# The first batch of a decoder layer with its projections in another order

## The chip, the cores and the metric

The kernel runs on one core of one Trainium2 chip. Its time is the device time of one execution in microseconds (us). Three timed runs of the kernel before gave 1556.1, 1555.15 and 1556.22; the median is 1556.1. One further execution was profiled: it took 1556.36, and the profile's span is 1554.6.

A core has five engines that run beside each other, each through its own list of instructions in order: TensorE (PE, matrix products; its weight loads are listed as PEld), VectorE (DVE), ScalarE (ACT), GpSimd (POOL) and SyncE (SP, which here issues most DMAs). Results of PE go to PSUM, and DVE or ACT carry them to SBUF.

## What is computed

A pre-norm decoder layer over `x` of 8 batches, 256 tokens, 1024 features: self-attention, cross-attention and a feed-forward network, each added to its input. The change touches only the self-attention of the first batch. Its weights are taken by their signs, and each output row is scaled by the mean absolute weight:

```python
def bitnet_linear(x, weight, scale_param):
    s = jnp.maximum(jnp.mean(jnp.abs(weight), axis=1), 1e-08)
    binary_w = jnp.sign(weight / s[:, None])
    y = jnp.einsum('bsi,oi->bso', x, binary_w)
    y = y * (s * scale_param)[None, None, :]
    return jnp.nan_to_num(y, nan=0.0, posinf=1000000.0, neginf=-1000000.0)

q = bitnet_linear(hidden_states, q_weight, q_scale)   # 32 heads of 32
k = bitnet_linear(hidden_states, k_weight, k_scale)   # 8 heads of 32, each used four times
v = bitnet_linear(hidden_states, v_weight, v_scale)
scores = jnp.einsum('bhqd,bhkd->bhqk', q, k) / np.sqrt(HEAD_DIM)
attn = jax.nn.softmax(scores, axis=-1)
out = jnp.einsum('bhqk,bhkd->bhqd', attn, v)
return bitnet_linear(out, o_weight, o_scale)
x = x + attention(layernorm(x))
```

## The kernel before

**Weight blocks.** The four weight matrices come in 20 blocks of 128 output rows by 1024 (512 KB): two of k, two of v, eight of q, eight of o. The list `blocks` (L243 to L262) gives their order, and "block 5" or "weight 5" means the sixth of that list. Before: k0, k1, q0, q1, v0, v1, q2 to q7, o0 to o7. Each block needs

- a load by SP (`weight_load`, L273): one DMA for k and v, four for q, eight for o. Eight buffers hold blocks (`room`); `after` says which later block takes the buffer of an earlier one, and `weight_next` issues that load after the earlier block's sum;
- a turn (`weight_turn`, L303): eight 128x128 transposes on PE into two PSUM banks, and two passes of ACT that write the signs;
- a sum (`weight_sum`, L292): a DVE reduction over 1024 columns with a small operation behind it, and three small operations on POOL that put the row's scale factor into a column of `scol`.

**Scale tables.** The outputs of q and k are scaled row by row from `scol` by ACT. Those of v and o need the factors along the free dimension: `scale_part` (L318) lets POOL multiply the identity by each column (`dg`, in its `ahead`), lets PE multiply ones by these (`ps_d`, L332) and lets DVE copy the result to `v_sc` or `o_sc` (L333).

**Projections.** A chunk is 128 outputs for 256 tokens: 16 matrix products over `xh` and `xl`, the upper and lower part of the normalised, transposed input. `first_chunk` (L414) makes a single chunk with its clean-up on DVE alone: five operations, six for k. `proj_T` (L386) makes two chunks as two parts; with the second, ACT scales both out of the PSUM bank into `y` (L406), and `nan_to_num` (L345) cleans up on DVE (two operations) and POOL (`tmp` L350, an addition L351), with a predicated copy on DVE (L355) that is not issued at once: `settle` (L172), called at each part, issues it two parts later. Three PSUM banks in rotation (`bank`, L107) serve turns, projections, tables and transposes; a bank is free again when its last reader is done.

**Steps.** A batch has eight steps, one for four heads. `step` (L676) issues the scores (PE, 16 products into four banks), the row maxima `nm` (DVE, L686), four times four transposes of the step before's probabilities with ACT's copies (`turned`, L518), and then the parts which `self_plan` (L1134) gives to this step; among them, by a budget in us that each part carries, come ACT's eight exponentials (L705). When the first four are issued, `over_sums(0)` is called, and after all eight `over_sums(1)`: a DVE reciprocal each, and then two heads divided by their sums. The table `BY` (L1112) says by whom: "D" is DVE, "P" is POOL. For the first batch it is DDDD, PPPD, PPPD, PPPP, PPPD, PPPD, DDDD, PPPD. A step ends with the product of the transposed probabilities of the step before with v (`po`, L581), which the step after it carries to `oh` and `ol`. Parts that have something to prepare (`ahead`) prepare it when the part in front of them is run, or at the start of the step if they are among its first two or are marked `soon`.

**The first batch** also holds the turning of the weights. Before the first step (from L1249): the loads of x and of eight blocks, the layernorm's statistics, turn 0, the layernorm (transposes L1268, casts L1270, subtractions L1273), turn 1, the sums 0 and 1, then k0, turn and sum 2, k1, turn and sum 3, q0, q1, and the load of the second batch's x. `self_plan` for batch 0 then gives the steps v, q2 to q7, the other turns, the tables, the second batch's layernorm (`ln_parts`, four parts, each with `xn` on DVE as its `ahead`, four transposes on PE, a cast on ACT and a subtraction `xl` on DVE) and the second batch's k, v and q0 to q3. The second batch's moments are prepared in pieces on DVE (`idle`, L125; run by a credit of time).

All five engines are under a hand-written order: each carries out its instructions as the program issues them.

Of the kernel before, what the change touches and what calls it, by code (L numbers as in the profile page):

```python
# [35 lines left out]
def decoder_layer(  # L36
# [24 lines left out]
    nc = tc.nc  # L61
# [3 lines left out]
    EC = E // P  # L65
# [170 lines left out]
    ps = bank([P, 20], "ps_p")  # L236
# [8 lines left out]
    def block(put, t, col, w, q=False, o=False):  # L245
        a = State()
        a.put, a.t, a.col, a.rows, a.q, a.o = put, t, col, w, q, o
        blocks.append(a)

    def columns(dst, t):  # L250
        return lambda e0: dst[:, e0 : e0 + 4, t * P : (t + 1) * P]

    for t in range(2):
        block(columns(kT_w, t), t, 8 + t, kw)
    for c in range(2):
        block(columns(qT_w[c], 0), c, c, qw, q=True)
    for t in range(2):
        block(columns(vT_w, t), t, 10 + t, vw)
    for c in range(2, EC):
        block(columns(qT_w[c], 0), c, c, qw, q=True)  # L260
    for t in range(EC):
        block(columns(oT_w, t), t, 12 + t, ow, o=True)  # L262

# [39 lines left out]
    def weight_turn(i):  # L303

        a = blocks[i]
        for h in range(2):
            nc.scalar.activation(
                a.put(4 * h), four_T(a.w[:, h * 512 : (h + 1) * 512], "ps_w"), AF.Sign
            )

    def weight_next(i):

        weight_turn(i)
        weight_sum(i)
        for k in after.get(i, []):
            weight_load(k)

    def scale_part(col0, n, dst, soon=False):  # L318

        box = {}  # L320

        def ahead():
            box["dg"] = wk_.tile([P, n, P], F32, tag="xn", name="dg", bufs=2)
            for k in range(n):
                nc.gpsimd.tensor_scalar_mul(
                    box["dg"][:, k, :], ident, scol[:, col0 + k : col0 + k + 1]
                )

        def main():
            ps = bank([P, n, P], "ps_d")  # L330
            for k in range(n):
                nc.tensor.matmul(ps[:, k, :], ones, box["dg"][:, k, :], start=True, stop=True)  # L332
            nc.vector.tensor_copy(dst, ps.rearrange("p k c -> p (k c)"))  # L333

        return Part(0.3 * n, main, ahead, soon)

    def weight(i):
        return Part(1.1, lambda: weight_next(i))
# [795 lines left out]
    def self_plan(b):  # L1134
        st = sts[b]
        if b == 0:
            nxt = sts[1]
            v0 = v_parts(st)
            ln, k, v = ln_parts(nxt, 1), k_parts(nxt), v_parts(nxt)
            return [  # L1140
                [weight(4), weight(5), v0[0], weight(6), weight(7)]
                + [scale_part(10, 2, v_sc), v0[1]],
                mixed(q_parts(st, 2) + q_parts(st, 4), [weight(8), weight(9), weight(10)]),
                [weight(11)] + q_parts(st, 6) + [weight(12)],
                [weight(13)] + ln[:2] + [weight(14)] + ln[2:],
                k[:1] + [weight(15)] + k[1:],
                mixed(v, [weight(16), weight(17)]),
                mixed(q_parts(nxt, 0), [weight(18), scale_part(12, 4, o_sc[:, 0:512], True)])
                + [weight(19)],
                mixed(q_parts(nxt, 2), [scale_part(16, 4, o_sc[:, 512:1024])]),  # L1150
            ]
        o = o_all(sts[b - 1])
        if b + 1 < B:
            nxt = sts[b + 1]
            ln = ln_parts(nxt, b + 1)
            return [
                q_parts(st, 4) + q_parts(st, 6),
                mixed(o[0], ln[:2]),
                mixed(o[1], ln[2:]),
                k_parts(nxt),  # L1160
                o[2] + v_parts(nxt),
                o[3],
                q_parts(nxt, 0),
                q_parts(nxt, 2),
            ]
        x0 = xts[0]
        ln = lnx_parts(x0)
        return [
            q_parts(st, 4) + q_parts(st, 6),
            o[0],  # L1170
            o[1],
            mixed(o[2], ln[:2]),
            mixed(o[3], ln[2:]),
            ctx_parts(x0, (act, dve)) + ckv_part(x0),
            cq_part(x0) + ckvT_part(x0),
            cqk_parts(x0, (dve, act)),
        ]
# [62 lines left out]
    with tc.manual_schedule(  # L1240
        engines={
            mybir.EngineType.PE,
            mybir.EngineType.DVE,
            mybir.EngineType.Activation,
            mybir.EngineType.Pool,
            mybir.EngineType.SP,
        }
    ):
        st = sts[0]  # L1249
        xb[0] = load_x(0)  # L1250
        for i in range(len(room)):
            weight_load(i)
        ln_moments(st, 0)
        need(st)
        weight_turn(0)
        st.xh = wk_.tile([P, EC, S], F32R, tag="xh", name="xh")
        st.xl = wk_.tile([P, EC, S], F32R, tag="xl", name="xl")
        lo = []
        for q in range(2 * TB):
            t, h = q // 2, q % 2  # L1260
            xn = wk_.tile([P, 512], F32, tag="p", name="xn0", bufs=4)
            nc.vector.tensor_scalar(
                xn, xb[0][t][:, h * 512 : (h + 1) * 512],
                st.mv[:, t, 0:1], st.rs[:, t : t + 1], ALU.subtract, ALU.mult,
            )
            ps = pss.tile([P, 4, P], F32, tag="pss", name="ps_t")
            for k in range(4):
                nc.tensor.transpose(ps[:, k, :], xn[:, k * P : (k + 1) * P], ident)  # L1268
            e4, t4 = slice(h * 4, (h + 1) * 4), slice(t * P, (t + 1) * P)
            nc.scalar.copy(st.xh[:, e4, t4], ps)  # L1270
            lo.append((st.xl[:, e4, t4], ps, st.xh[:, e4, t4]))
        for a in lo:
            nc.vector.tensor_sub(*a)  # L1273
        weight_turn(1)
        for i in range(2):
            weight_sum(i)
        for i in range(2):
            for k in after.get(i, []):
                weight_load(k)
        st.kT = wk_.tile([P, 2, S], F32, tag="kT", name="kT", bufs=2)  # L1280
        st.qT = wk_.tile([P, EC, S], F32, tag="qT", name="qT", bufs=2)
        for i in range(2):
            first_chunk(
                st, lambda e: kT_w[:, e, i * P : (i + 1) * P], 8 + i, st.kT[:, i, :], K_SCALE
            )
            weight_next(2 + i)
        for i in range(2):
            first_chunk(st, lambda e: qT_w[i][:, e, :], i, st.qT[:, i, :])
        xb[1] = load_x(1)

        prev = None
        for kind, sts_, plan, loads, extra, n in (
            (Self, sts, self_plan, self_loads, self_extra, EC),
            (Cross, xts, cross_plan, cross_loads, cross_extra, XH // 4),
        ):
            for b in range(B):
                ps_ = plan(b)
                for p in ps_:
                    queue.extend(p)
                for c in range(n):  # L1300
                    loads(b, c)
                    prev = step(kind(sts_[b], c), prev, len(ps_[c]), extra(b, c))


        pairs = [(fb, f) for fb in fbs for f in range(NF)]
        acs = {}

        def hidden_next(n):
            acs[n] = hidden(*pairs[n])

        prev.prev.early()
        pTs = [turned(p) for p in prev.p]
        prev.prev.late()
        fw.late = None
        hidden_next(0)
        prev.weighted(pTs)
        hidden_next(1)
        prev.early()
        prev.late()
        ffn_load_end()  # L1320
        fw.late = wt.tile([P, 2 * RC, W], F32, tag="vw", name="late")
        settle()
        settle()
        lag = 2
        for n in range(2, len(pairs) + lag):
            fb, f = pairs[n] if n < len(pairs) else (None, n)
            if fb is not None:
                hidden_next(n)
                if fb.i == 0 and f == 3:
                    x_leave(xts[B - 1])  # L1330
                elif idle:
                    idle.pop(0)()
                if fb.i + 1 < NB:
                    if f == 6:
                        ffn_x(fbs[fb.i + 1])
                    if f == 8:
                        hp = head_parts(fbs[fb.i + 1])
                        queue.extend(hp)
                        queue[0].ahead()
                    if 9 <= f < 9 + len(hp):  # L1340
                        run_part()
            m = n - lag
            down(*pairs[m], *acs.pop(m))
            if fb is not None and fb.i and 2 <= f < 2 + BT:
                tail(fbs[fb.i - 1], f - 2)
        for j in range(BT):
            tail(fbs[NB - 1], j)
# [34 lines left out]
```

## Time and profile before

| | value |
|---|---|
| median of three runs | 1556.1 us |
| the profiled execution | 1556.36 us |
| its span | 1554.6 us |
| PE busy in the span | 1510.9 us (97%) |
| DVE busy | 964.1 us (62%) |
| ACT busy | 799.8 us (51%) |
| POOL busy | 404.7 us (26%) |
| HBM read and written | 65.44 MB and 25.17 MB |

Steps of the first batch in that execution, by the start of their scores on PE and of their maxima on DVE (timeline):

| step | scores | maxima |
|---|---|---|
| 0 | 26.41 | 27.87 |
| 1 | 42.22 | 44.21 |
| 2 | 58.15 | 59.43 |
| 3 | 67.96 | 71.22 |
| 4 | 83.82 | 85.93 |
| 5 | 93.67 | 96.19 |
| 6 | 104.55 | 107.11 |
| 7 | 115.88 | 120.40 |
| second batch, 0 | 127.08 | 128.25 |

The page cuts the span into 40 slices of 38.9 us and gives each engine's busy share in tenths; the first batch lies in the first three and a bit. The first table's shares are means over the whole kernel, of which the first batch is a twelfth.

### The profile page before, as it was taken

What the parts mean: (1) busy time and instruction counts of PE and PEld (TensorE: products, weight loads), DVE (VectorE), ACT (ScalarE), POOL (GpSimd) and SP (SyncE); (2) the same over time, 40 slices, a digit from 0 to 9 for tenths busy, and PEclk for the clock granted to TensorE, in tenths of its full rate; (3) what the DMA queues carried; (4) which work ended last, traced back from release to release, by engine and by line L of the source; (5) the groups of instructions that cost most, each with busy time, mean ns of one, the idle gap of its engine ahead of it and who ended that gap; (6) DMA issues with size and microseconds to landing.
All of it is one profiled execution on the core that took longest, in us unless ns stands there. A gap on an engine that the chain in (4) does not pass through costs nothing.

```text
span 1554.6 us, 25703 instructions
## 1 busy us (share of the span) xinstructions
PE 1510.9 (97%) x9494; PEld 1014.8 (65%) x9494; DVE 964.1 (62%) x1880; ACT 799.8 (51%) x2448; POOL 404.7 (26%) x491
## 2 busy tenths in 40 slices
PE   6899999999999999999999999999999999999998
PEld 5777888788878786777778776544444444444443
DVE  7878999999989898766676665343233233423322
ACT  4677898989888888755565666311101111111110
POOL 2555443445354534022221111100020002001102
PEclk9989999999999999999999999999999999999999
DMA  8430020101020141211453311110001002000001
GB/s 233 67 82 26 18 69 28 55 29 67 17 69 29 60 150 44 86 42 61 154 187 132 113 61 77 48 54 0 0 41 68 1 0 108 0 1 27 28 0 54
DMA packets 65612, 92.78 MB, mean 60 GB/s; under 512 B 40218, under 2 KB 46160, under 8 KB 65360
## 3 DMA queue, kind: packets, MB, share of 16 engines
q1 hardware_dynamic: 60880, 74.37, 15.2%
q0 software_dynamic: 4608, 16.78, 2.7%
q8 instruction: 75, 1.23, 0.3%
q14 instruction: 49, 0.40, 0.1%
HBM read 65.44 MB, written 25.17 MB: 58 GB/s over the span
## 4 chain that ended last, share of the span: by engine, by line
PE 78%; DVE 10%; ACT 6%; DMA 2%; issue 1%; POOL 1%; SPq 1%; POOLq 0%; DVEq 0%; ACTq 0%
PE ps_h L1034 19%; PE ps_z L1078 9%; PE ps_pt L522 9%; PE ps_q L397 6%; PE ps_o L490 5%; ACT p L705 4%; PE s L619 4%; PE ps_p L1008 4%; PE po L642 4%; PE ps_o L1097 3%; PE s L543 3%; PE po L581 3%; DVE nm L686 2%; PE ps_o L659 2%; PE ps_q L848 2%; PE ps_qk L863 2%
## 5 line engine op out<-in xcount | busy, mean ns | idle before, releaser
L705 ACT ACTIVATE p<-s,nm 128x256 f32<-128x256 f32 x768 | 357.9, 517 | 0.4 <-DVE nm L686 0.4
L526 ACT COPY pT<-ps_pt 128x512 f32<-128x512 f32 x384 | 198.6, 598 | 178.1 <-PE ps_pt L522 177.3
L1046 ACT ACTIVATE sg<-ps_h,b_col 128x512 f32<-128x512 f32 (+1 forms) x88 | 59.7, 678 | 413.5 <-PE ps_h L1034 413.5
L686 DVE TENSOR_REDUCE nm<-s 128x2 f32<-128x512 f32 x384 | 237.3, 677 | 9.9 <-PE s L619 6.8
L1047 DVE SCALAR_TENSOR_TENSOR sg<-ps_h,b_col,sg 128x512 f32<-128x512 f32 (+1 forms) x88 | 64.9, 738 | 272.2 <-ACT sg L1046 272.2
L522 PE MATMUL ps_pt<-ident,p 128*128 128x128 f32 x1536 | 195.7, 278 | 4.8 <-DVE xl L343 3.2
L522 PEld LDWEIGHTS ps_pt<-ident,p 128*128 128x128 f32 x1536 | 164.4, 141 | 45.6 <-issue 25.5
L705 ACT ACTIVATION_READ_ACCUMULATOR p<-s,nm 128x1 f32 x768 | 190.9, 249 | 0.0
L1107 POOL TENSOR_TENSOR x2t<-x2t,y 128x512 f32<-128x512 f32 x32 | 40.6, 1267 | 480.3 <-DVE y L1105 480.3
L1078 PE MATMUL ps_z<-ac,u_sb 128*128 128x512 f32 x336 | 157.7, 593 | 0.0
L397 PE MATMUL ps_q<-xh,qT_w 128*128 128x256 f32 x496 | 121.8, 287 | 0.0
L397 PE MATMUL ps_q<-xl,qT_w 128*128 128x256 f32 x496 | 118.9, 281 | 0.0
L674 POOL TENSOR_TENSOR x1t<-x1t,y 128x256 f32<-128x256 f32 x64 | 47.5, 764 | 234.6 <-DVE y L667 234.6
L1078 PEld LDWEIGHTS ps_z<-ac,u_sb 128*128 128x128 f32 x336 | 61.9, 190 | 68.8 <-issue 68.8
L490 PE MATMUL ps_o<-oT_w,oh 128*128 128x512 f32 x256 | 105.9, 414 | 0.0
L350 POOL TENSOR_SCALAR tmp<-y 128x512 f32<-128x512 f32 x78 | 57.2, 733 | 183.7 <-DVE y L499 106.4
L490 PE MATMUL ps_o<-oT_w,ol 128*128 128x512 f32 x256 | 101.0, 395 | 0.0
L566 DVE TENSOR_SCALAR p<-p,sm 128x256 f32<-128x256 f32 x252 | 90.1, 414 | 8.0
L397 PEld LDWEIGHTS ps_q<-xh,qT_w 128*128 128x128 f32 x496 | 93.3, 188 | 1.6
L397 PEld LDWEIGHTS ps_q<-xl,qT_w 128*128 128x128 f32 x496 | 93.4, 188 | 0.0
L1034 PE MATMUL ps_h<-pT,w_ffn 128*128 128x512 f32 (+1 forms) x184 | 88.7, 577 | 0.0
L1034 PE MATMUL ps_h<-late,w_ffn 128*128 128x512 f32 (+1 forms) x184 | 88.7, 577 | 0.0
(159 smaller groups left out, 2737.0 us busy)
## 6 DMA issues: line engine op xcount, KB each, us to landing
xs<-in_x_dram SPq DMA_DIRECT2D x32, 512.0 KB, 4.1
x<-xs POOLq DMA_DIRECT2D x16, 512.0 KB, 3.0
x1t<-x SPq DMA_DIRECT2D x16, 512.0 KB, 5.2
c<-in_ctx_dram SPq DMA_DIRECT2D x16, 512.0 KB, 3.8
x<-x1t POOLq DMA_DIRECT2D x16, 512.0 KB, 3.8
x2t<-x SPq DMA_DIRECT2D x16, 512.0 KB, 5.8
out_dram<-x2t SPq DMA_DIRECT2D x16, 512.0 KB, 2.6
w<-in_L_attn_q_weight_dram SPq DMA_DIRECT2D x32, 128.0 KB, 5.9
```

Of the source, the lines that this page charges most:

```text
L397: nc.tensor.matmul(ps[:, i, :], w(i, e), x_[:, e, :], start=(e == 0 and x_ is st.xh), stop=(e == EC - 1 and x_ is st.xl),)
L490: nc.tensor.matmul(ps, o_[c // 4][:, c % 4, t * P : (t + 1) * P], oT_w[:, c, h * 512 : (h + 1) * 512], start=(c == 0 and o_ is st.oh), sto ...
L522: nc.tensor.transpose(ps[:, k, t * P : (t + 1) * P], p[:, t, k * P : (k + 1) * P], ident)
L526: nc.scalar.copy(pT, ps)
L566: nc.vector.tensor_scalar_mul(p, p, self.sm[:, t, j : j + 1])
L619: nc.tensor.matmul(s[2 * i + j][:, t, :], st.cqk[p0 : p0 + XD, 2 * c + i, t * P : (t + 1) * P], st.ckv[p0 : p0 + XD, :], start=True, stop= ...
L642: nc.tensor.matmul(self.po[XD * j : XD * (j + 1), i, :], self.st.ckvT[:, k, :], pTs[2 * i + j][:, k, :], start=(k == 0), stop=(k == TB - 1),)
L686: nc.vector.tensor_reduce(nm[:, j, :], s[j], AX.X, ALU.max, negate=True)
L705: nc.scalar.activation(cur.p[j][:, t, :], s[j][:, t, :], AF.Exp, bias=nm[:, j, t : t + 1], accum_out=cur.sm[:, t, j : j + 1],)
L1034: nc.tensor.matmul(ps[h * n : h * n + n], v1_of(r, i, f, n), fb.pT[:, r, h * w_ : (h + 1) * w_], start=(r == 0), stop=(r == RC - 1),)
L1047: nc.vector.scalar_tensor_tensor(sg[:m], hs[0][:m], bg, sg[:m], ALU.add, ALU.mult)
L1078: nc.tensor.matmul(fb.zs[r], fw.u2[f // 4][:n, f % 4, r * P : (r + 1) * P], ac[:n], start=(k == 0), stop=(k == NF - 1 and COPIES < 2),)
```

## The change

It has five parts.

1. The list of blocks is put in another order: k0, q0, q1, v0, v1, q2, q3, k1, q4 to q7, o0 to o7. Loads follow this order.
2. Before the first step only k0 and q0 are projected. The sum of block 0 (k0) moves ahead of the layernorm. Blocks 2 and 3 (q1, v0) are turned there, and block 2 is summed. The load that takes block 2's buffer is issued in step 0.
3. `weight_next` is split, so that sums and loads can be issued apart from turns (`weight_free`). In step 0, `turn_4` turns block 4, sums 3 and 4 and issues the loads behind them; blocks 5 and 6 are turned there, and their sums are issued at the end of the step (`sums`).
4. The parts are dealt out to the steps anew: q1 to step 0, the second k chunk to step 1, q4 and q5 to step 2, q6 and q7 to step 3 with the second batch's layernorm; the o blocks are turned a step later in part, and the second half of the o table is the last part of step 7.
5. The scale tables are copied from PSUM by ACT in place of DVE.

```diff
-    for t in range(2):
-        block(columns(kT_w, t), t, 8 + t, kw)
-    for c in range(2):
-        block(columns(qT_w[c], 0), c, c, qw, q=True)
+    def q_blocks(*chunks):
+        for c in chunks:
+            block(columns(qT_w[c], 0), c, c, qw, q=True)
+
+    K, V, Q = [0, 7], [3, 4], [1, 2, 5, 6, 8, 9, 10, 11]
+    block(columns(kT_w, 0), 0, 8, kw)
+    q_blocks(0, 1)
     for t in range(2):
         block(columns(vT_w, t), t, 10 + t, vw)
-    for c in range(2, EC):
-        block(columns(qT_w[c], 0), c, c, qw, q=True)
+    q_blocks(2, 3)
+    block(columns(kT_w, 1), 1, 9, kw)
+    q_blocks(4, 5, 6, 7)
...
+    def weight_free(i):
+        for k in after.get(i, []):
+            weight_load(k)
+
     def weight_next(i):
-
         weight_turn(i)
         weight_sum(i)
-        for k in after.get(i, []):
-            weight_load(k)
+        weight_free(i)
...
-            nc.vector.tensor_copy(dst, ps.rearrange("p k c -> p (k c)"))
+            nc.scalar.copy(dst, ps.rearrange("p k c -> p (k c)"))
...
+            def turn_4():
+                weight_turn(4)
+                weight_free(2)
+                for i in V:
+                    weight_sum(i)
+                    weight_free(i)
+
+            def sums():
+                for i in Q[2:4]:
+                    weight_sum(i)
+                    weight_free(i)
+
             return [
-                [weight(4), weight(5), v0[0], weight(6), weight(7)]
-                + [scale_part(10, 2, v_sc), v0[1]],
-                mixed(q_parts(st, 2) + q_parts(st, 4), [weight(8), weight(9), weight(10)]),
-                [weight(11)] + q_parts(st, 6) + [weight(12)],
-                [weight(13)] + ln[:2] + [weight(14)] + ln[2:],
-                k[:1] + [weight(15)] + k[1:],
-                mixed(v, [weight(16), weight(17)]),
-                mixed(q_parts(nxt, 0), [weight(18), scale_part(12, 4, o_sc[:, 0:512], True)])
-                + [weight(19)],
-                mixed(q_parts(nxt, 2), [scale_part(16, 4, o_sc[:, 512:1024])]),
+                [Part(2.0, lambda: q_chunk(1)), Part(0.9, turn_4), v0[0]]
+                + [Part(0.9, lambda i=i: weight_turn(i)) for i in Q[2:4]]
+                + [scale_part(10, 2, v_sc), v0[1], Part(0.0, sums)],
+                mixed(q_parts(st, 2), [weight(8), weight(7)])
+                + [Part(2.0, lambda: k_chunk(1)), weight(9)],
+                [weight(10)] + mixed(q_parts(st, 4), [weight(11)]),
+                q_parts(st, 6) + ln[:2] + [weight(12)] + ln[2:],
+                mixed(k, [weight(13), weight(14)]),
+                mixed(v, [weight(15), weight(16)]),
+                mixed(q_parts(nxt, 0), [weight(17), scale_part(12, 4, o_sc[:, 0:512], True)])
+                + [weight(18)],
+                mixed(q_parts(nxt, 2), [weight(19)]) + [scale_part(16, 4, o_sc[:, 512:1024])],
             ]
...
         weight_turn(0)
+        weight_sum(0)
+        weight_free(0)
...
         weight_turn(1)
-        for i in range(2):
-            weight_sum(i)
-        for i in range(2):
-            for k in after.get(i, []):
-                weight_load(k)
+        weight_sum(1)
+        weight_free(1)
...
-        for i in range(2):
+        def k_chunk(i):
             first_chunk(
                 st, lambda e: kT_w[:, e, i * P : (i + 1) * P], 8 + i, st.kT[:, i, :], K_SCALE
             )
-            weight_next(2 + i)
-        for i in range(2):
+        def q_chunk(i):
             first_chunk(st, lambda e: qT_w[i][:, e, :], i, st.qT[:, i, :])
+        k_chunk(0)
+        q_chunk(0)
+        for i in (2, 3):
+            weight_turn(i)
+        weight_sum(2)
         xb[1] = load_x(1)
```

## The prediction

> **What bounds the kernel now.** I read the page's slices first, then the busy time by stretch, then what TensorE (PE) waited for up to 160 us, then the timelines of DVE, ACT and POOL over the first batch. "Step c" is head group c of the first batch; "block" is a slice of weights in the plan's order.
>
> ```profile
> PE   6899999999999999999999999999999999999998
> DVE  7878999999989898766676665343233233423322
> ...
> 160.00:180.00 20.00, 20.00 (x180) 16.79 (x179) 17.42 (x38) 15.81 (x53) 9.57 (x9) 1.00 0.07 29
> ```
>
> After 160 us PE is full, and the diff touches nothing there. What counts is the first batch. Its steps' scores start (timeline of PE) at 26.41, 42.22, 58.15, 67.96, 83.82, 93.67, 104.55 and 115.88, the second batch's first at 127.08; a shift of that last one is the change in time.
>
> ```profile
> 30.00:40.00 10.00, 5.98 (x41) 5.32 (x41) 8.60 (x20) 5.87 (x21) 3.79 (x14) 0.91 0.79 178
> ...
> 70.00:80.00 10.00, 5.89 (x38) 4.32 (x35) 9.93 (x17) 8.28 (x24) 4.51 (x9) 0.79 0.08 12
> ...
> 34.70:38.20 3.50, 0.48 (x2) 0.30 (x2) 3.17 (x8) 1.17 (x4) 1.73 (x5) 1.00 0.64 99
> 38.20:41.60 3.40, 3.16 (x15) 3.15 (x15) 1.28 (x5) 0.00 (x0) 0.80 (x4) 0.51 0.73 114
> ```
>
> Columns: length, then busy PE, weight load, DVE, ACT, POOL, then PE's granted clock. In 70 to 80 DVE is full and PE is not: there the bound is DVE. After PE's idle stretch at 34.7 the clock is 0.51.
>
> ```profile
> PE ps_d L332 <- POOL dg L325: 3.3, 2, 3.0
> PE ps_t L163 <- DVE xn L155: 2.9, 3, 2.2
> PE ps_w L163 <- ACT y L406: 1.9, 2, 1.4
> ...
> 24.75 0.15 DVE L298 TENSOR_SCALAR s<-total 128x1 f32<-128x1 f32 x1
> 24.82 0.28 DVE L428 TENSOR_SCALAR qT<-y 128x256 f32<-128x256 f32 x1
> ...
> 27.87 2.48 DVE L686 TENSOR_REDUCE nm<-s 128x2 f32<-128x512 f32 x4
> ...
> 121.33 2.38 POOL L325 TENSOR_SCALAR dg<-ident,scol 128x128 f32<-128x128 f32 x4
> 123.66 3.10 POOL L559 TENSOR_TENSOR p<-p,sm 128x512 f32<-128x512 f32 x3
> ```
>
> The longest waits: 3.0 us for v's scale table, 2.2 for the layernorm, 1.4 for a PSUM bank held by y. q0's clean-up (24.82) stands behind a weight sum, so the first maxima come at 27.87. In step 7 the second o-table's dg (121.33) stands ahead of POOL's multiplications.
>
> **Prices** (spacings in the timelines). PE: chunk 2.0 (45.11 to 47.12), turn 0.8, scores 1.1, four transposes of p 1.9, po 1.0. DVE: sum 1.3 (15.78 to 17.09), clean-up of one chunk 1.65 (24.82 to 26.46), of K 1.8, maxima 2.4. ACT: exp 0.45, casts of a turn 1.0. POOL: p 1.02, dg 0.6, a block's scol 0.8. A DVE pair of p takes 1.9 beside POOL (50.99).
>
> **Prologue.** Block 0's sum falls into DVE's wait for rs (idle 1.15 before 10.25): 9.1 to 10.4, so xn starts 0.2 later; nothing else. q0 replaces k1 in the DMA queue: its last piece lands at 13.2 today (chain), earlier by k1's half megabyte then, and its turn is at 14.3. k0 on PE 15.3 to 17.3, q0 to 19.3; its scale factor is there by 18.3, so y at 19.75, clean-up after k0's 19.8 to 21.35. Scores 21.4: 5.0 earlier, but two chunks (4.0 of PE) are still owed.
>
> **Step 0.** Sum of block 2, then maxima 22.75 to 25.15; q1's clean-up to 26.75, v's sums to 29.5, p of pair 0 to 30.8, pair 1 to 32.1. POOL's dg is ready at 31.75 instead of 38.4, since only v's two sums stand ahead. PE loses some 1.4 and 0.8 to the banks of turns 5 and 6; table 32.3. No row shows ACT copying 128x256 from PSUM to a table: the cast of oh (0.37) and the copy of 128x512 (0.60) bound it, I take 0.4, off DVE's 0.42. v's second half ends at 34.25; DVE has v's part to 36.2, the two sums put off to 38.9. Scores of step 1 at 34.25 (8.0 earlier), maxima only at 38.9 (5.3 earlier).
>
> **Step 1.** The maxima, not PE, set the pace: exps 39.6 to 44.15, with turn 8's casts between, then y of q2, q3. Block 7's turn needs the bank that this y holds (the 1.4 us wait above, same rotation of banks): q's second chunk ends at 41.95, y at 45.0, so the wait grows to 3.05. Then k1 must follow its own turn at once: casts to 46.45, chunk to 48; its y waits on ACT for scol till 50.0. DVE: 2.4 maxima, 0.7 of v, three sums 4.0, pair 1.9, q 0.8, q's predicated copy 0.7, moments 2.1, K 1.8, waits 1: step 2's maxima at 54.4 (5.0 earlier; scores 50).
>
> **Step 2.** Two sums, a pair, one q: maxima of step 3 at 64.0, 7.2 earlier, with a sum and q6, q7's pass (2.8 of DVE) still owed.
>
> **Step 3** holds q6, q7 and the layernorm. Its p are "PPPP": POOL gets four multiplications (4.1) at the reciprocal, 68.5, then q's tmp 0.65 and add 1.3: 74.55. q's predicated copy is issued on DVE two parts after q, that is behind the first xl and ahead of the second xl, third xn, block 12's sum and fourth xn. DVE reaches it at 71.0 and stands 3.5 us; today no q ends in this step. All that is queued on DVE waits, and PE for it: idle 71.5 to 76.45, last transposes at 79. Maxima of step 4: 82.9, only 3.0 earlier, with two sums (2.6) owed.
>
> **SP's queue.** q6 and q7 now go behind the second batch's x and behind the sums of blocks 2 and 3 (22.7, 28.1); they are turned from 53 on. The load of block 13 waits for a sum put off, 37.6, and is turned in step 4; that of block 19 for block 15's sum, 99.7: eight DMAs (4.46 at 92.25) and 2.4 to land, 107, turned at 117. None is on the path, which costs nothing as long as these 10 us and more last.
>
> **The clock** goes down in both. The row: 2.23 us of idle ended at 74.29, and 74.30 to 82.00 ran at 0.60, the po after it took 1.86 for 1.0. The Trainium skill (TensorE: Matmul & The Clock Gate, Part 1: The HAM clock gate) speaks of half rate after at least one idle window of about 3.4 us. By its rule neither that stop nor the one before 37.72 would cost anything unless a whole window were idle, and step 7's term below would be 0 or 1.7; the trace shows a drop after 2.2 us, so it decides, and the term stays.
>
> **Steps 4 to 6.** Step 4 has a sum and turn more than today (10.3 to 11.5 of DVE): maxima of step 5 at 94.4, of step 6 at 104.5 (today 107.11). Step 6 keeps DVE busy for 13.29 today; without the o-table's copy (0.64, spacing 0.56) 12.7: maxima of step 7 at 117.2, 3.2 earlier, with one sum owed. ACT copies the table in 0.60 (row of pT) where it has room.
>
> **Step 7** now ends with the second o-table, and its dg is made ahead only when q's second half starts. From the maxima N: first four exps N+2.5, reciprocal N+2.95, POOL two p to N+5.0, block 19's scol to 5.8, third p (needs all exps, casts of turn 19 between them) to 6.85, dg to 9.25, PE's table N+9.5, po, scores N+10.5. Today it is 127.08 - 120.40 = N+6.7: 3.8 lost. PE itself is through its chunks at 120.0, so it stands some 4 us.
>
> **Sum.** 117.2 + 10.5 = 127.7 against 127.08: +0.6. PE's stop of 4 us brings a stretch at half clock; the row (po 1.86 for 1.0, then scores 2.0 for 1.1) gives +1.7, bounds 0 (none: the 1.41 stop at 50.05 left the clock at 1.0) and 1.7; I take 1.5, as 4 us is longer than the 2.2 that sufficed. +2.1. The profiled execution took 1556.36 (span 1554.6), 0.26 above the median; so 1556.1 + 2.1 = 1558.2.
>
> **Rivals.** *Lead lost (slower):* the same place in step 7, if DVE's lead there is gone. In step 0 a half-clock v chunk (38.45 to 41.6 shows 0.41 for 0.28, +1.2) or more waits in step 1 would do it. With N at 120.4 the scores come at 130.9, +3.8, clock 1.7: 1561.6; it decides from N of 118 on (+1.4 and 1.7). For it: DVE is full already, the sums are only shifted, and a lead of 5 at step 1 shrinks to 3. Against: three table copies left DVE.
>
> *Lead kept (faster):* the predicated copy does not stand, if the exps of step 3 and thus POOL run earlier than I have it. N is then 113.7, scores 124.2, PE stops about 1 us only and the clock stays: -2.9; with 1.5 less at the banks of turns 5 to 7: -4.4, 1551.7. For it: 3.0 at v's table goes in any case, and PE has 10.8 us of work in step 3 to cover the layernorm. Against: POOL's order is fixed by the program, and 6 us of it stand between reciprocal and copy.
>
> *Scores no earlier:* if the change does not do what it says, because q0's clean-up is late as today or q0 lands late, the first maxima stay near 27.9 and only the table copies (0.42 and 0.56) leave DVE before step 7: N 119.4, scores 129.9, +2.8, clock 1.5: 1560.4. Against: at 21.35 nothing stands ahead of q0's clean-up, and q0 has over 1 us to spare. I count it to lead lost.
>
> **Numbers.** A measurement of this kernel tells about 0.2% (3.1 us) from no change. Chances: my case 0.43, nearly all of it between 1553.0 and 1559.2; lead lost 0.37; lead kept 0.20. My case alone: N uncertain by 1.5 and the clock's term 0 to 1.7, so 1555.2 to 1559.9. The range runs on to both rivals with the unknown costs, 1551.5 to 1563.
>
> **What would show it.** Right: first scores near 21.4; PE waiting on dg near 31 for under 1.5 us; PE waiting on y L406 3 us near 45; DVE waiting for POOL at a predicated copy some 3.5 us in step 3; PE waiting on dg about 4 us at the end of step 7, at half clock after it. Wrong: no wait on dg near 121, or step 3 shorter than 14 us, then faster; second batch's scores after 130, then slower.

## The result, and the profile after

The changed kernel takes 1561.21 us, the median of six runs (1560.83 to 1563.52), against 1555.92 before (six runs): a ratio of 1.0037, interval 1.0025 to 1.0049, or 5.3 us slower. Its profiled execution took 1561.12 with a span of 1559.3, that of before 1556.36 and 1554.6.

The page's slices of the changed kernel:

```profile
PE   7798999999999999999999999999999999999998
...
DVE  7886899999999899766676665343133223423322
...
PEclk9898999999999999999999999999999999999999
```

PEclk is the clock that PE was granted, in tenths of full speed. Behind the first four slices PE's row is the same as before. Its second slice (39 to 78 us) fell from 8 to 7 and its fourth (117 to 156) from 9 to 8, and in both the clock is down to 8 tenths; DVE's fourth fell from 8 to 6. Only the first slice gained. So the loss is in two places of the first batch.

| step | scores before | after | maxima before | after | maxima predicted |
|---|---|---|---|---|---|
| 0 | 26.41 | 21.31 | 27.87 | 22.47 | 22.75 |
| 1 | 42.22 | 34.00 | 44.21 | 39.01 | 38.9 |
| 2 | 58.15 | 51.66 | 59.43 | 54.68 | 54.4 |
| 3 | 67.96 | 61.47 | 71.22 | 64.36 | 64.0 |
| 4 | 83.82 | 81.91 | 85.93 | 83.41 | 82.9 |
| 5 | 93.67 | 91.94 | 96.19 | 94.87 | 94.4 |
| 6 | 104.55 | 101.64 | 107.11 | 105.68 | 104.5 |
| 7 | 115.88 | 113.55 | 120.40 | 118.83 | 117.2 |
| second batch, 0 | 127.08 | 131.15 | 128.25 | 133.25 | scores 127.7 and clock |
| second batch, 1 | 138.81 | 144.13 | 139.98 | 145.30 | |

The lead of 6.9 at step 3's maxima shrinks to 2.5 in that step (19.05 us long, 14.71 before), and in step 7 it turns into a loss of 4.1 at the second batch's first scores. At the scores of its next step the loss is 144.13 - 138.81 = 5.3, the whole result; the profiled executions, 4.8 apart, differ less, as the rest of the kernel gave back 0.6 in this pair. What PE waited for, up to 160 us, in the changed kernel (total, times, longest):

```profile
PE ps_d L339 <- POOL dg L332: 5.2, 2, 4.9
...
PE ps_w L163 <- ACT y L413: 3.9, 2, 3.4
PE ps_t L163 <- DVE xn L155: 3.7, 2, 3.1
```

The same three names as before, with other sizes: the wait for a table has gone from step 0 (3.0) to step 7 (4.9), that for y's bank has grown from 1.4 to 3.4, that for the layernorm from 2.2 to 3.1. Behind each, PE runs at half clock (in step 3 from 72.39 on, ahead of the longest wait: PE had waited 2.3 there for an earlier xl). Busy time by stretch (length, PE, weight load, DVE, ACT, POOL, PE's granted clock):

```profile
41.80:45.20 3.40, 0.03 (x1) 0.00 (x0) 2.25 (x7) 3.39 (x12) 2.71 (x6) 0.98 0.69 107
45.20:48.40 3.20, 3.16 (x14) 2.93 (x15) 3.20 (x5) 1.20 (x2) 3.03 (x3) 0.50 0.63 99
...
77.30:82.00 4.70, 4.09 (x28) 2.11 (x28) 2.99 (x5) 1.17 (x2) 0.81 (x3) 0.50 0.01 3
121.40:126.40 5.00, 0.05 (x2) 0.01 (x1) 3.69 (x8) 3.60 (x13) 4.38 (x8) 0.72 0.00 0
126.40:133.20 6.80, 6.58 (x41) 3.84 (x41) 0.55 (x2) 0.96 (x2) 3.98 (x5) 0.50 0.00 0
133.20:145.30 12.10, 12.10 (x117) 10.86 (x114) 8.04 (x18) 9.22 (x29) 3.17 (x4) 0.97 0.01 2
```

**Step 7**: PE has 0.05 us of work in 5.00, then runs 6.80 us at 0.50. The timelines of POOL and PE of the changed kernel (start, us, operation, idle before it and its releaser) show why:

```profile
121.86 2.04 POOL L566 TENSOR_TENSOR p<-p,sm 128x512 f32<-128x512 f32 x2 [2.09 <-DVE sm L563]
...
124.62 1.04 POOL L566 TENSOR_TENSOR p<-p,sm 128x512 f32<-128x512 f32 x1
125.65 2.85 POOL L332 TENSOR_SCALAR dg<-ident,scol 128x128 f32<-128x128 f32 x4
```

```profile
126.39 0.79 PE L339 MATMUL ps_d<-dg,ones 128*128 128x128 f32 x2 [4.95 <-POOL dg L332]
```

POOL takes dg only after the multiplications of p, which wait for step 7's exponentials. Before, dg stood ahead of them (121.33, with p at 123.66). PE's last chunk ends at 121.44, so nothing is left to cover the wait.

**Step 3**, DVE of the changed kernel:

```profile
72.36 0.68 DVE L350 TENSOR_TENSOR xl<-ps_t,xh 128x512 fp32r<-128x512 f32 x1
75.41 0.73 DVE L362 COPY_PREDICATED qT<-fin,y 128x512 f32<-128x512 uint8 x1 [2.38 <-POOL qT L358]
76.03 0.68 DVE L350 TENSOR_TENSOR xl<-ps_t,xh 128x512 fp32r<-128x512 f32 x1
76.63 0.54 DVE L155 TENSOR_SCALAR xn<-xs,mv,rs 128x512 f32<-128x512 f32 x1
```

DVE, which was the bound of this stretch before, stands 2.38 us at q6 and q7's predicated copy; the layernorm's next xl and xn are queued behind it, and PE waits 3.1 for that xn. The copy waits for POOL:

```profile
68.93 4.41 POOL L566 TENSOR_TENSOR p<-p,sm 128x512 f32<-128x512 f32 x4 [1.85 <-DVE sm L563]
73.42 0.61 POOL L357 TENSOR_SCALAR tmp<-y 128x512 f32<-128x512 f32 x1
74.12 1.26 POOL L358 TENSOR_TENSOR qT<-qT,tmp 128x512 f32<-128x512 f32 x1
```

In the kernel before, q6 and q7 were projected in step 2. Their copy fell into step 3 as well, but POOL's addition was done at 71.11, and DVE did not wait:

```profile
74.85 0.73 DVE L355 COPY_PREDICATED qT<-fin,y 128x512 f32<-128x512 uint8 x1
```

### The profile page after: what moved, and what is told of

Read it like the earlier page. It is cut to its first block, busy times and chain, and to the rows that moved or that the text cites. A ratio compares the mean times of both kernels' runs of the same rounds, so it can differ in the third digit from the quotient of the medians.

```text
span 1559.3 us, 25699 instructions
## 1 busy us (share of the span) xinstructions
PE 1511.9 (97%) x9494; PEld 1016.2 (65%) x9494; DVE 963.9 (62%) x1877; ACT 799.1 (51%) x2451; POOL 404.3 (26%) x491
## 4 chain that ended last, share of the span: by engine, by line
PE 82%; DVE 9%; ACT 6%; POOL 2%; issue 1%; DMA 0%; SPq 0%; POOLq 0%; DVEq 0%; ACTq 0%
PE ps_h L1041 19%; PE ps_z L1085 9%; PE ps_pt L529 9%; PE ps_q L404 6%; PE ps_o L497 5%; ACT p L712 4%; PE s L626 4%; PE ps_p L1015 4%; PE po L649 3%; PE ps_o L1104 3%; PE s L550 3%; PE po L588 3%; PE ps_v L471 2%; DVE nm L693 2%; PE ps_q L855 2%; PE ps_qk L870 2%
```

## The experiments

Two theories stood against each other. **Order**: the loss sits in two places where work is queued wrongly, the second o table as the last part (step 7) and q6 and q7 ahead of the layernorm (step 3); undo both and the early scores win. **DVE**: the first batch is bound by DVE, the early scores only put its work off, and the loss stays wherever the parts stand. All kernels but three (runs 4, 8 and 9) start from the changed one. Runs 1 to 4, runs 5 to 8 and runs 9 and 10 were each measured on one chip, together with the kernel before: 1556.27 (33 runs), 1556.10 (33) and 1556.23 (18). Each ratio is to that kernel. The changed kernel was not measured beside them, so what is given back of its 5.3 us, and any difference between two of the three groups, is uncertain by what chips differ in (the kernel before: 1555.92 to 1556.27).

**1. The o table ahead again.** Block 19 goes back to step 6, and the table stands among step 7's parts:

```diff
-                + [weight(18)],
-                mixed(q_parts(nxt, 2), [weight(19)]) + [scale_part(16, 4, o_sc[:, 512:1024])],
+                + [weight(18), weight(19)],
+                mixed(q_parts(nxt, 2), [scale_part(16, 4, o_sc[:, 512:1024])]),
```

> The changed kernel with one thing undone: weight 19 goes back to the end of step 6 and the second o-table to the middle of step 7, so that its dg stands ahead of POOL's multiplications. Order theory (the loss sits where an in-order queue holds PE; here 4.9 us of waiting on dg and the half clock behind it): step 7's maxima come 1.3 later (block 19's sum in front), near 120.2, the second batch's first scores 6.7 after them as in the kernel before, near 126.9, at full clock; no wait on dg over 1.5 us there. Time 1555.5 to 1556.5. DVE theory (DVE's total of work bounds the first batch, the place of a wait means little): DVE has as much to do as in the changed kernel, the second batch's scores move by 1 us at most, time 1560 to 1561.

1558.62 (1557.77 to 1560.43), ratio 1.0015 [1.0006, 1.0024]: 2.6 of the 5.3 are back, between the two theories. DVE's timeline in this run:

```profile
118.44 1.22 DVE L300 TENSOR_REDUCE total<-w 128x1 f32<-128x1024 f32 x1
...
120.06 1.22 DVE L300 TENSOR_REDUCE total<-w 128x1 f32<-128x1024 f32 x1 [0.22 <-issue]
...
121.39 2.47 DVE L693 TENSOR_REDUCE nm<-s 128x2 f32<-128x512 f32 x4
```

The two sums, of blocks 18 and 19, now stand ahead of the maxima, which start at 121.39 (118.83 in the changed kernel), and dg needs the second: PE still waits 2.4 for it. The order theory had the maxima at 120.2; DVE has no lead left that would pay for the second sum.

**2. The predicated copy later.** q6 and q7's copy is put back twice more, which is four parts later, so that it is issued in step 4, behind the layernorm's last operations:

```diff
+    def held(f, n):
+        return f if n == 0 else (lambda: later.append(held(f, n - 1)))
+
-        later.append(finish)
+        later.append(held(finish, hold))
...
-                q_parts(st, 6) + ln[:2] + [weight(12)] + ln[2:],
+                q_parts(st, 6, hold=2) + ln[:2] + [weight(12)] + ln[2:],
```

> The changed kernel with the predicated copy of q6 and q7 issued four parts later, in step 4, so that the layernorm's operations on DVE don't stand behind POOL's four multiplications. Order theory: DVE does not stop from 73.0 to 75.4, the third layernorm transposes move from 77.3 to about 74.2, step 4's scores from 81.9 to about 78.8; the wait on dg in step 7 stays near 4.9. Time 1557.5 to 1558.5. DVE theory: 2.4 us of idle DVE are filled, but the copy is done later all the same, 0.7; less than 1.5 is left at the second batch: 1559.7 to 1561.

1559.57 (1557.57 to 1561.03), ratio 1.0019 [1.001, 1.0028]: 1.6 back, again between the two theories. DVE no longer stands: xn starts at 73.00 instead of 76.63, step 3 lasts 16.40 instead of 19.05, and PE's waits in this run are

```profile
PE ps_d L339 <- POOL dg L332: 5.2, 2, 5.0
...
PE ps_t L163 <- DVE xn L155: 2.0, 2, 1.0
```

The wait for xn has shrunk from 3.1 to 1.0, that for dg is untouched. Step 7's maxima come 2.2 earlier (116.63), the second batch's scores 2.3 (128.85) and those behind them 3.5 (140.59). This execution lies 1.6 under its kernel's median, so the trace shows more than the median does.

**3. Both edits together.**

```diff
-                q_parts(st, 6) + ln[:2] + [weight(12)] + ln[2:],
+                q_parts(st, 6, hold=2) + ln[:2] + [weight(12)] + ln[2:],
...
-                + [weight(18)],
-                mixed(q_parts(nxt, 2), [weight(19)]) + [scale_part(16, 4, o_sc[:, 512:1024])],
+                + [weight(18), weight(19)],
+                mixed(q_parts(nxt, 2), [scale_part(16, 4, o_sc[:, 512:1024])]),
```

> Both edits together. Order theory: the two gains add up, as each removes a stop of its own: second batch's scores near 123.8, time 1552 to 1553.5, faster than the kernel before by 2.5 to 4. DVE theory: not under 1558.

1555.61 (1554.81 to 1557.94), ratio 0.9997 [0.9988, 1.0006]. The two places make up all of the loss: mended together they give back 5.6 by medians, more than singly (2.6 and 1.6, in sum 4.2). But with both mended, scores that start 5 us earlier gain nothing over before. Each theory was half right.

**4. The table copies alone**, on the kernel before: the third suspect, ACT's copies.

```diff
-            nc.vector.tensor_copy(dst, ps.rearrange("p k c -> p (k c)"))
+            nc.scalar.copy(dst, ps.rearrange("p k c -> p (k c)"))
```

> The kernel before with one part of the change alone: ACT in place of DVE copies the scale tables from PSUM. Order theory: the wait of step 7's transposes for the bank that DVE copies late (1.0 us) goes, and DVE is 0.56 and 0.42 ahead at two places: faster by 0.5 to 1.5, time 1554.5 to 1555.5. DVE theory: faster by DVE's own share, 1.0 at most before step 7: 1555 to 1555.9. If ACT's queue holds the copy back, slower by up to 0.6.

1557.67 (1555.18 to 1557.89), ratio 1.0004 [0.9996, 1.0013]: no effect that can be told. Two of its eleven runs took 1555.2 and nine 1557.2 to 1557.9. The two show a mean granted clock of 0.996, the nine 0.994 to 0.995, so more time at half clock goes with the longer runs; what decides it is not shown. The trace is of one of the two (1555.25): there step 7's maxima come 0.95 earlier, PE waits 1.0 for dg, and the second batch's scores still start 0.96 earlier (126.12).

**5. The sums of step 0 later** (run 3, with the sums of blocks 5 and 6 behind the maxima of step 1 instead of ahead of them):

```diff
-                + [scale_part(10, 2, v_sc), v0[1], Part(0.0, sums)],
-                mixed(q_parts(st, 2), [weight(8), weight(7)])
+                + [scale_part(10, 2, v_sc), v0[1]],
+                [Part(0.0, sums)] + mixed(q_parts(st, 2), [weight(8), weight(7)])
```

> Both edits of before (table back, predicated copy later), and the two sums put off (blocks 5 and 6) put off further: behind step 1's maxima instead of ahead of them. It asks whether the maxima set the pace in step 1. Lead theory (DVE's early lead is work owed; what DVE must do by step 7 is the bound, so a PE wait in step 1 costs nothing of its own): step 1's maxima move from 39.4 to about 36.8, the wait of turn 7 for the bank from 3.4 to under 1.2, but step 2's maxima move by at most 1 and the time by less than 0.7 against both edits alone (1555.6). Wait theory (PE's 3.4 us and the half clock behind it are lost): scores of step 2 some 3 earlier and the time 1553 or less.

1554.5 (1552.88 to 1556.58), ratio 0.999 [0.9981, 0.9998], 1.1 under run 3 (measured on another chip): between the two expectations. The maxima of step 1 start at 36.72 instead of 39.41, and the wait for y's bank is 1.4:

```profile
PE ps_w L163 <- ACT y L416: 1.9, 2, 1.4
```

So the wait at y's bank shrinks when the sums go, and the clock, at 0.50 behind that wait in run 3, stays at 1.00 up to 71.85. But most of the gain is shifted again: counted from the first turn of each trace (9.99 here, 8.90 in run 3), step 1's maxima are 3.8 earlier (26.73 for 30.51), step 2's 1.0 (45.13 for 46.17), since the two sums have to be done in between. From there the lead grows to 2.3 at the second batch's scores (114.83 for 117.15), which is 1.2 in the traces' own times (124.82 for 126.05), near the 1.1 of the medians. Why it grows is not shown, and neither theory is borne out.

**6. q6 and q7 away from the layernorm** (with the table of run 1), at the end of step 2:

```diff
-                [weight(10)] + mixed(q_parts(st, 4), [weight(11)]),
-                q_parts(st, 6) + ln[:2] + [weight(12)] + ln[2:],
+                [weight(10)] + mixed(q_parts(st, 4), [weight(11)]) + q_parts(st, 6),
+                ln[:2] + [weight(12)] + ln[2:],
```

> The changed kernel with the second o-table back in the middle of step 7 and with q6 and q7 back in step 2, away from the layernorm, predicated copies as in the change. Lead theory: the stop of DVE in step 3 goes as with the late copy, since q's cleaning is ahead of POOL's four multiplications; step 2 is longer by its 4 us of PE, step 3 shorter; step 4's maxima near 80.5 to 82, time 1554.8 to 1556.2, like both edits. Cover theory (q6 and q7 beside the layernorm are worth having for the PE work they give): step 3 has PE idle for most of its 12 us, half clock in it, time 1557 to 1558.5.

1557.77 (1556.73 to 1559.27), ratio 1.0011 [1.0002, 1.002]. By time this is worse than run 3. But in the profiled execution the first weight block landed late: the first turn starts at 11.11, in run 3 at 8.90. Counted from there, step 4's maxima come at 71.9 against 72.1 in run 3, and the second batch's scores at 117.2 in both. DVE's stop has not gone but moved: DVE stands 2.66 us at 69.66, in step 2, at the copy of q4 and q5. In step 3 PE is busy for 7.05 of 11.27 us, more than the cover theory had. The time falls into that theory's range, the trace speaks against it: whether PE needs q6 and q7 beside the layernorm stays open.

**7. Two sums on ACT** (run 3, with the sums of blocks 18 and 19, those of step 7's backlog, taken from DVE):

```diff
-        nc.vector.tensor_reduce(total, a.w, AX.X, ALU.add, apply_absolute_value=True)
+        if i >= 18:
+            nc.scalar.activation(a.w, a.w, AF.Abs, accum_out=total)
+        else:
+            nc.vector.tensor_reduce(total, a.w, AX.X, ALU.add, apply_absolute_value=True)
```

> Both edits of before, and ACT in place of DVE sums the last two blocks (18 and 19, one pass over 1024 columns with accumulation, estimated from four exps of 256 columns at 0.45 as 1 to 1.8 us each). Lead theory: step 6 goes from 14.8 us of DVE to some 12.5, step 7's maxima from 118.0 to about 115.7, the wait for dg in step 7 from 2.4 to under 1, and the half clock after it goes: 1551.5 to 1553.5. If DVE is not the bound there, or ACT becomes it: 1555 or more.

1553.41 (1551.67 to 1554.9), ratio 0.9978 [0.9969, 0.9987], 2.2 under run 3 (measured on another chip). Step 6 and the stretch up to the second batch's maxima, in run 3 and then here (columns as above):

```profile
103.24:118.01 14.77, 13.09 (x122) 11.07 (x120) 13.85 (x31) 10.34 (x30) 7.34 (x17) 1.00 0.26 81
118.01:127.21 9.20, 7.41 (x57) 5.69 (x58) 5.68 (x12) 5.57 (x20) 6.99 (x12) 0.81 0.00 0
```

```profile
106.44:118.41 11.97, 10.95 (x105) 9.08 (x104) 11.32 (x30) 11.19 (x33) 6.19 (x14) 1.00 0.28 95
118.41:127.70 9.29, 8.57 (x79) 6.66 (x78) 5.68 (x14) 6.47 (x23) 7.81 (x16) 1.00 0.00 0
```

DVE is full in both (13.85 of 14.77, 11.32 of 11.97), and step 6 is shorter by 2.8 where DVE has 2.5 less; ACT takes that up. PE's wait for dg falls to 0.4, and the clock stays at 1.00 where run 3 had 0.81. In step 6 DVE is the bound. It is not so in every step: in step 5 of the changed kernel PE has no idle time at all,

```profile
94.87:105.68 10.81, 10.81 (x107) 9.52 (x106) 10.26 (x21) 8.97 (x27) 6.23 (x11) 1.00 0.63 98
```

and step 5 takes the same 10.81 in this run; in step 4 PE is busy for all of its 11.46 us.

**8. The same two sums on ACT, on the kernel before** (edit as in 7).

> The kernel before with the sums of blocks 18 and 19 on ACT. Lead theory: step 6 keeps DVE busy for 12.9 of 13.3 us, so it gets shorter, by 1 to 1.5 as PE's own work there is 11.8; time 1554.5 to 1555.5. If DVE is not the bound: 1556 or more. Beside the run before it shows what the new order is worth once that bound is eased in both: the difference of the two.

1555.18 (1553.7 to 1556.17), ratio 0.9993 [0.9984, 1.0002]. In the trace step 6 takes 11.50 instead of 13.29, but the time goes down by 0.9 only, and the interval takes in no change. With this relief in both, the new order with its two places mended (run 7, on the same chip) is 1.8 better.

**9. The early scores alone, on the kernel before**: k0 and q0 ahead of the first scores, k1, q1 and two sums as parts of step 0.

```diff
-        for i in range(2):
-            first_chunk(
...
+        k_chunk(0)
+        q_chunk(0)
+        weight_turn(1)
+        weight_turn(3)
...
-                [weight(4), weight(5), v0[0], weight(6), weight(7)]
+                [Part(0.0, rest_sums), Part(2.0, lambda: k_chunk(1)), Part(2.0, lambda: q_chunk(1))]
+                + [weight(4), weight(5), v0[0], weight(6), weight(7)]
```

> The kernel before with the headline of the change alone: k0 and q0 ahead of the first scores, the second k chunk, the second q chunk and the sums of their blocks as parts of step 0; order of blocks, other steps, tables and DVE's copies as before. Lead theory (the early scores are DVE work put off, not saved): step 0's maxima some 5 earlier, near 22.5 for a first turn at 8.6, but the sums of v come no earlier than at 30 to 33.5 and step 1's maxima stay within 1 of 44.2; time 1555.3 to 1557. If early scores are a gain in themselves: step 1's maxima near 40, time 1551.5 to 1553.

1555.8 (1555.06 to 1557.1), ratio 0.9997 [0.9988, 1.0007]: no effect. Step 0 from its maxima to those of step 1, here and in the kernel before:

```profile
23.90:45.96 22.06, 17.68 (x124) 15.64 (x125) 18.23 (x43) 8.93 (x27) 5.86 (x22) 0.85 0.75 170
```

```profile
27.87:44.21 16.34, 12.00 (x91) 10.56 (x90) 12.58 (x28) 7.92 (x25) 4.74 (x16) 0.90 0.74 158
```

The step begins 4.0 earlier and is 5.7 longer: DVE has 18.23 us of work in it where it had 12.58. The difference, 5.65, is near what was put off: K's clean-up 1.8, q1's 1.65, two sums 2.6. But PE's work has grown as much, from 12.00 to 17.68 (two chunks, 4.0 at full clock, were put off too), so this run does not show which of the two sets the length of step 0. (The first turn was at 10.11 here, at 8.64 before, so measured from there step 1's maxima are 0.3 later than before.) The early scores shift the work of both and save none.

**10. What helped, together**: runs 3, 5 and 7.

```diff
+                [Part(0.0, sums)] + mixed(q_parts(st, 2), [weight(8), weight(7)])
...
+                q_parts(st, 6, hold=2) + ln[:2] + [weight(12)] + ln[2:],
...
+                + [weight(18), weight(19)],
+                mixed(q_parts(nxt, 2), [scale_part(16, 4, o_sc[:, 512:1024])]),
...
+            nc.scalar.activation(a.w, a.w, AF.Abs, accum_out=total)
```

> What the runs so far say is worth having, in one kernel: the change with the second o-table back, the predicated copy late, the two sums behind step 1's maxima, and the sums of blocks 18 and 19 on ACT. Lead theory: the gains of 1.1 (sums later) and 2.2 (ACT sums), both measured against both edits at 1555.6, add up: 1551.8 to 1553, faster than the kernel before by 3 to 4. If one takes the other's place: 1553.4 or more.

1551.88 (eight runs, 1550.35 to 1553.47), ratio 0.9972 [0.9962, 0.9982]: faster than before by 4.3 and than the change by 9.3 (on another chip). PE's table in step 7 now waits 0.43:

```profile
117.82 2.25 PE L342 MATMUL ps_d<-dg,ones 128*128 128x128 f32 x8 [0.43 <-POOL dg L335]
```

## Why the prediction was right, and where it was short

The forecast was 1558.2, the time 1561.21: the direction was right, but +2.1 was too small against +5.3. The time lies outside the 1555.2 to 1559.9 of the prediction's own case and in the band that it gave to lead lost, with N (step 7's maxima) at 118.83, past the 118 that it named. The places and their mechanisms were named ahead of the result; that the time still lies inside the full range, 1551.5 to 1563, is owed to its having been drawn over the rivals.

- **First scores, steps 0 to 3**: right. First scores 21.31 (21.4 predicted), maxima of steps 1 to 3 within 0.4. Near 31 PE does not wait for dg at all, but 0.39 for ACT's pass of a turn (under 1.5 for dg was said):

```profile
31.42 0.73 PE L339 MATMUL ps_d<-dg,ones 128*128 128x128 f32 x4 [0.39 <-ACT qT_w L311]
```

- **The wait for y's bank**: 3.4 for 3.05, right. That PE then runs 3.20 us at 0.50 was not in the sum.
- **DVE's stand in step 3**: the right place and releaser, 2.38 instead of 3.5 (73.0 to 75.4). DVE reached the copy 2.0 later than said, in part because q's clean-up just ahead of it took longer: beside POOL's multiplications its two DVE operations took 1.15 and 1.26. POOL was done 0.8 later than said, and step 4's maxima came 0.5 later. The prediction's "today no q ends in this step" is not quite so: q6 and q7's copy stood in it before too, but without a wait.
- **Steps 4 to 6: the N of the sum**: short. Step 5 took 10.81 for 10.1, step 6 13.15 for 12.7; with the 0.5 from step 3, N came 1.63 later. For step 5 the prediction gives no working for taking 0.8 off today's 10.92; its sums there are of DVE, but PE is busy for all of the 10.81. Step 6 was costed as today's 13.29 less the table's copy. Those 13.29 are the step's length, not DVE's busy time as the prediction says (12.94), and 0.32 us of the 0.56 that the copy left free went into a wait for POOL at a predicated copy (116.89).
- **Step 7**: the mechanism held (dg behind p, PE standing 4.95 where "some 4" was said).
- **What follows PE's stop in step 7, the clock term above all, is the term that was furthest off**: 1.5, with 1.7 as its upper bound, taken from a stop of 2.23 us. N + 10.5 = 129.33, but the scores came at 131.15 (1.8 later), and the step behind them took 12.98 for 11.73 (1.25 more): 3.1 us. Of these 0.4 is dg itself (2.85 for the 2.4 of the sum). The other 2.6 is work of PE at half clock: the end of the table's products 0.53, po 0.87 and, in the step behind, the scores 0.94 and the transposes 0.30. The prediction had priced po and the scores alone:

```profile
127.40 1.95 PE L339 MATMUL ps_d<-dg,ones 128*128 128x128 f32 x6 [0.22 <-POOL dg L332]
129.28 1.94 PE L588 MATMUL po<-pT,v 128*32 128x256 f32 x16
131.15 2.09 PE L550 MATMUL s<-kT,qT 32*128 32x256 f32 x16
```


The sum with the measured terms is 0.6 + 1.6 + 3.1 = 5.3; they are taken from the same two traces, so that it comes out is no further proof. The reading that a lead of several us at the scores is worth little was right, and run 9 shows it by itself. On DVE's side: step 0's maxima come 5.4 earlier, but K's second clean-up (1.8), q1's (1.65) and a sum (1.3) are put off, 4.75 of DVE; the true lead is 0.65. At step 4 it is 2.5 less two sums owed (2.6): nothing.

What the two misplacements cost is shown by runs 1 to 3. That DVE bounds step 6 is shown by run 7. That it bounds the first batch as a whole is not shown: PE has no idle time in steps 4 and 5, and in run 9 PE's work grows with DVE's. Not settled: how the loss of step 3 splits between DVE's stand and the half clock behind it, and run 6.

## What to carry to other kernels

Count a lead on the bounding engine net of the work that it still owes: a stage whose maxima start 5.4 us earlier because 4.75 us were put off has won 0.65. Look up which engine bounds each stage: here it changes from step to step. Before a part is moved to the end of a stage, look in every in-order queue at what its preparation and its late clean-up will stand behind, since whoever is queued behind them waits as well. A stop of PE can cost more than its length: to price the half clock behind it, count all the work of PE that falls into it and that others wait for.

## What the hardware showed

**The clock.** A stop of 2.23 us (before) was followed by a stretch at 0.60, one of 3.4 by 3.20 us at 0.50, one of 4.95 by 6.80 at 0.50; one of 1.41 (before) left it at 1.00. Finer windows show more. The clock does not follow the start or the end of a stop: in the kernel before it fell at 75.81, 1.5 us after the stop of 2.23 was over, so that row does not show "a drop after 2.2 us", as the prediction reads it; in the changed kernel it fell at 123.59, 2.1 us into the stop of 4.95. Each trace has its changes on a grid of 3.41 us: the stretches at half clock last 3.41, 6.83 or 10.24 us, and the two behind these stops were equally long. First the kernel before, then the changed one (columns as above):

```profile
72.40:75.81 3.41, 1.36 (x11) 1.18 (x12) 3.41 (x8) 2.90 (x11) 0.00 (x0) 1.00 0.00 0
75.81:86.05 10.24, 7.84 (x49) 4.30 (x47) 6.50 (x13) 5.15 (x16) 5.66 (x10) 0.50 0.38 58
```

```profile
120.18:123.59 3.41, 1.26 (x11) 1.06 (x9) 2.91 (x6) 3.41 (x14) 1.73 (x2) 1.00 0.00 0
123.59:133.83 10.24, 7.22 (x43) 4.48 (x44) 3.11 (x6) 2.36 (x8) 6.63 (x11) 0.50 0.00 0
133.83:137.24 3.41, 3.41 (x31) 3.25 (x30) 2.91 (x6) 3.02 (x9) 0.00 (x0) 1.00 0.00 0
```

The Trainium skill (TensorE: Matmul & The Clock Gate, Part 1: The HAM clock gate) speaks of at least one idle window of about 3.4 us. The length agrees with these traces; that the window must be idle does not, as PE was busy for 1.36 and 1.26 us of the two above. It was busy for 2.01 us of the one that holds the stop of 1.41 (48.50 to 51.92), and the clock stayed. Where the grid lies differs from trace to trace, so the same stops can cost differently: the layernorm of step 3 had 10.24 us of half clock behind it in the kernel before and 3.41 in run 4 (80.73 to 84.14).

**DVE beside POOL.** In the changed kernel q6 and q7's clean-up ran while POOL multiplied p: 1.15 and 1.26 us for one operation of 128x512 each, where the same forms took 0.41 each at 92.89 and 93.23, with POOL idle from 92.82 to 93.46.

**The first landing.** The first weight block is asked for at 3.25 to 3.27 in every trace; its first turn starts between 8.59 and 11.11 (before 8.64, changed 8.88, runs 1 to 4 from 8.59 to 9.09, runs 5, 6, 7 and 9 from 9.99 to 11.11, run 8 8.89, run 10 10.53). The runs don't tell whether the chip, the loads beside it or chance makes the difference. Two us there are as much as most effects here, so the times in a single trace have to be counted from its first turn.
